# Spline weights from four terms an element; the down weights formed in the feed-forward stage; softmax reciprocals behind the next unit's minima

## The chip, the cores and the metric

One core of a Trainium2 chip runs the whole kernel in one launch. The metric is the device time of an execution in microseconds; a profile is one execution recorded by the hardware profiler. Everything is float32.

## The reference

For four sequences of 512 tokens with 512 features, a layer norm gives `xn`. Two branches read it and both are added to `x`: causal attention with 16 heads of 32 features and a linear position bias (ALiBi), and a gated feed-forward block whose three weights are not stored but interpolated.

```
xn = (x - mean) / sqrt(var + eps)
q, k, v = xn @ W + b                       # 16 heads of 32
p   = softmax(q k^T / sqrt(32) + slope_h * distance, causal)
att = (p v) @ Wo + bo
gate_w, up_w, down_w = catmull_rom(control points)   # 2048x512, 2048x512, 512x2048
ffn = (silu(xn @ gate_w^T) * (xn @ up_w^T)) @ down_w^T
out = x + att + ffn
```

Every spline sample is a sum of four neighbouring control points, each times a cubic of the position. A control point spans about 129 samples, so long runs of a weight row are one cubic. The kernel uses this: it multiplies small factored weights (called `wT` for gate and up, and `dR` and `dM` inside `dRM` for down) with reduced features, which it lays out in DRAM as `table` and loads as `feat`.

## The kernel before, in words

The program is written out as a straight line; each engine carries out its own instructions strictly in the written order (`in_order` ties them so). DMAs are issued by SP (SyncE) and, for the `table` rows, by POOL; an issue that has to wait for an engine or for an earlier transfer holds up all that stands behind it on that queue.

**Attention stage (0 to 388 us).** The work is a list `units` of 64: sequence b, head group hg of four heads, query block i of 128. In iteration n, `scores(units[n])` has PE form four score tiles (L865) in the four PSUM banks of pool `ps_s`, and DVE add the distances and take the row minimum of each (L878, tile `low`); the blocks i = 0 and i = 1 of a group share one set of banks, so their scores are made together. ACT takes the exponentials and their sums (L894). In iteration n+1, `normalize` has DVE form the reciprocals of the four sums (L907, tile `inv`) and POOL multiply the tile by them (L909). In iteration n+2, `swap` transposes part of the tile on DVE (L937) and SP moves it (L945, `move`). In iteration n+3, `turn` transposes the rest on PE (L922), ACT copies it out (L923), and after the group's last block `values` multiplies with v (L966). The banks of `ps_s` come free with DVE's minima, so PE's next scores wait for these. Between them stand the lists `items` (projections L798 and L837, output projections L482, layouts) and `small` (layer norm statistics).

Ahead of `scores(n)` stands `normalize(n-1)`: DVE's reciprocals, which need the sums of ACT, come before the minima of unit n.

**The weights.** `row_weight_steps` forms `wT` in this stage on DVE, as eight terms (`NCG`) for gate and for up: a table `coef` times the control points, a product (L646) and a sum (L649) of 1024 elements a partition each. The points come by four broadcast DMAs a term. `down_steps` forms `dR` and `dM` after that, from five and four terms (L690, L693), with three loads in flight in the space of `feat[0]`. The helper `some_weights` hands out these steps by a budget of microseconds an iteration, half ahead of `items` and half behind; the last step runs at 286 us.

**Feed-forward stage (from 388 us).** The strings in `plans` give the order by hand, one string a sequence. In the first, `G q` and `U q` are the gate and up products of a quarter q on PE (L1135, into the four banks of `ps_g`), `V q` is an up product into the four banks of `ps_o`, `P r` an output projection of the last sequence (L482, one bank of `ps_o`; DVE adds bias and residual, L489, and SP stores it, L492). G is followed by ACT (L1150). U and V are followed by four DVE products a quarter (L1157, tile `inner`), four POOL copies (L1158, tile `made`), and then on SP two exchange DMAs (L1162) and a few small ones (L1167). `F q` loads a quarter of the next `feat` (L549), `X` lets POOL issue rows. In the second string `m0:8` are the first moment products of sequence 0 on PE (L1182); they go into the `ps_o` banks, which V3's four DVE products leave. `down_values` (L1236) is the first to need `dR`.

Of the kernel before, what the change touches and what calls it, by code (L numbers as in the profile page):

```python
# [18 lines left out]
P = 128  # L19
# [29 lines left out]
NCV = 5  # L49
NX = 9 + 4  # L50

COPIES = (1, 1, 4, 1)
NW, NW4 = 11, 4
NST = NW4 + 1

DOWN_STEPS = [("v", lo, hi, c) for lo, hi in ((0, 5), (5, 9)) for c in range(NCV)]
DOWN_STEPS += [("m", 0, NB, c) for c in range(4)]

# [276 lines left out]

def own_points(parts, points):


    values = parts[:, :, :, :9].transpose(0, 4, 3, 1, 2)
    values = values.reshape(P, 9, 2, P // 2, NCD)  # L340
    moments = parts[:, :, :, 9:].transpose(3, 4, 0, 1, 2)
    moments = moments.reshape(P, NB, 2, P // 2, NCD)
    strip = np.broadcast_to(points[:, None, None], (NB, Q32, 9, P, NCD)).reshape(values.shape)
    group = np.broadcast_to(points[None], (P, NB, P, NCD)).reshape(moments.shape)
    own = {}
    for kind, a, number, n in (("v", values, strip, NCV), ("m", moments, group, 4)):
        hit = (a != 0.0).any(axis=3)
        first = np.where(hit.any(axis=3), hit.argmax(axis=3), 0)
        first = np.minimum(first, NCD - n)[:, :, :, None, None] + np.arange(n)
        first = np.broadcast_to(first, (*a.shape[:4], n))  # L350
        few = np.take_along_axis(a, first, axis=4)
        assert np.count_nonzero(few) == np.count_nonzero(a)
        shape = (*a.shape[:2], P, n)
        own[kind] = few.reshape(shape), np.take_along_axis(number, first, axis=4).reshape(shape)
    steps = [[a[:, lo:hi, :, c].reshape(-1) for a in own[k]] for k, lo, hi, c in DOWN_STEPS]
    return *(np.concatenate(a) for a in zip(*steps)),
# [20 lines left out]
_coef = _coef.reshape(NB, NB, P, NCG, 2, Q32).transpose(3, 1, 5, 0, 4, 2)  # L377
COEF = single(_coef.reshape(NCG, P, NB, 2, P))
# [20 lines left out]
def block_kernel(  # L399
# [152 lines left out]
    with ExitStack() as att:  # L552
# [63 lines left out]
        def row_weight_steps(first_down):  # L616
            size = NB * 2 * P
            shaped = lambda a: a.rearrange("p (q x n) -> p q x n", q=NB, x=2)
            spare = [
                feat[0].rearrange("p c h s -> p (c h s)")[:, k * size : (k + 1) * size]  # L620
                for k in range(4)
            ]
            temps = [wd[:, :size], wd[:, size : 2 * size]]
            tabs, points = {}, {}

            def load(c):
                def go():
                    tabs[c], points[c] = (shaped(a) for a in spare[c % 2 * 2 :][:2])
                    nc.sync.dma_start(out=tabs[c], in_=coef[c])
                    for k in range(NB):  # L630
                        strip = slice(k * Q32, (k + 1) * Q32)
                        nc.sync.dma_start(
                            out=spare[c % 2 * 2 + 1][strip],
                            in_=rowpts[c, k].partition_broadcast(Q32),
                        )

                return go

            def term(c, w):
                to = wT[:, :, 2 * w : 2 * w + 2, :]  # L640
                tmp = shaped(temps[w]) if c else to

                def times():
                    own = points[c].rearrange("p (w q) x n -> p w (q x) n", w=2)[:, w]
                    own = own.unsqueeze(2).to_broadcast([P, NB, 2, P])
                    nc.vector.tensor_tensor(tmp, tabs[c], own, ALU.mult)  # L646

                def plus():
                    nc.vector.tensor_tensor(to, to, tmp, ALU.add)  # L649

                return [times, plus] if c else [times]

            steps = [(0.0, load(0)), (0.0, load(1))]
            for c in range(NCG):
                for w in range(2):
                    steps += [(1.2, half) for half in term(c, w)]
                if c + 2 < NCG:
                    steps.append((0.0, load(c + 2)))
                elif c + 2 == NCG:
                    steps += first_down  # L660
            return steps


        def down_steps():
            size = 5 * P
            spare = feat[0].rearrange("p c h s -> p (c h s)")
            given, at = [], 0
            for _, lo, hi, _ in DOWN_STEPS:
                given.append((at, (hi - lo) * P))
                at += P * (hi - lo) * P  # L670

            def load(n):
                def go():
                    at, width = given[n]
                    for k, source in enumerate((downtab, downpts)):
                        to = spare[:, (n % 3 * 2 + k) * size :][:, :width]
                        part = source[at : at + P * width].rearrange("(p x) -> p x", p=P)
                        nc.sync.dma_start(out=to, in_=part)

                return go  # L680

            def term(n):
                kind, lo, hi, c = DOWN_STEPS[n]
                width = given[n][1]
                to = (dR if kind == "v" else dM)[:, lo:hi].rearrange("p a n -> p (a n)")
                tmp = wd[:, n % 2 * size :][:, :width] if c else to
                tab, own = (spare[:, (n % 3 * 2 + k) * size :][:, :width] for k in range(2))

                def times():
                    nc.vector.tensor_tensor(tmp, tab, own, ALU.mult)  # L690

                def plus():
                    nc.vector.tensor_tensor(to, to, tmp, ALU.add)  # L693

                return [times, plus] if c else [times]

            steps = [(0.0, load(n)) for n in range(3)] + [(2.4, lambda: None)]
            for n in range(len(DOWN_STEPS)):
                steps += [(0.9, half) for half in term(n)]
                if n + 3 < len(DOWN_STEPS):  # L700
                    steps.append((0.0, load(n + 3)))
            return steps


# [331 lines left out]
        first_down, *rest = down_steps()  # L1036
        weights = deque(row_weight_steps([first_down]) + rest)
# [27 lines left out]
        for _ in range(2):  # L1065
            weights.popleft()[1]()

        def some_weights(us):
            while weights and us > 0.0:
                cost, step = weights.popleft()  # L1070
                step()
                us -= cost

        for n in range(len(units) + LAG):
            u = units[n] if n < len(units) else None
            old = units[n - LAG] if n >= LAG else None
            if 0 <= n - 1 < len(units):
                normalize(units[n - 1])
            if u:
                scores(u)  # L1080
# [23 lines left out]
            for step in items[n]:  # L1104
                step()
            for step in small[n]:
                step()
# [255 lines left out]
```

## Time and profile before

| | |
|---|---|
| median of 3 runs | 544.58 us (543.7 to 544.58) |
| the profiled execution | 543.63 us, of which 541.4 us are the span from first to last instruction |
| mean granted TensorE clock | 0.993 |
| busy: PE, DVE, ACT, POOL | 530.3, 352.8, 296.0, 243.8 us |
| attention stage, feed-forward stage | 0 to 388 us, 388 to 541 us |
| terms for gate and up (L646, L649) | 30 DVE instructions, 37.5 us, at 44 to 185 us |
| terms for down (L690, L693) | 25 DVE instructions, 19.1 us, at 186 to 287 us |
| loads of the down tables (`feat<-in_downtab`, `feat<-in_downpts`) | 28, of 256 or 320 KB |
| reciprocals (L907) | 64, 10.9 us, and 29.1 us of idle DVE before them until ACT's sums |

A "busy" PE is not PE at its peak: matmuls are pipelined and their ends are modelled, and a matmul that waits for a bank can lie inside a busy stretch. Idle time of another engine costs only where PE then waits for it. In a timeline, instructions of one kind in a row are merged (x4), and the bracket tells how long the engine sat idle before and what ended that.

### The profile page before, as it was taken

Reading aid. Unit: us, or ns where it says so; the run is one execution under the profiler, and the core shown is the slowest. Engines: PE = TensorE matmul, PEld = TensorE weight load, DVE = VectorE, ACT = ScalarE, POOL = GpSimd, SP = SyncE. Lnnn points to the kernel's source line nnn. Section 1 sums busy time; section 2 is a strip of 40 time slices with the busy share of each in tenths; the row PEclk is TensorE's granted clock in tenths of the full one; section 3 lists DMA queues with packets and bytes.
Section 4 is the critical chain, followed back from the end, with each engine's and each line's share of the span. In section 5 each row is a group of like instructions: output and inputs, shape, how many; then the busy total and the mean of one; then the engine's idle time right before and its main releaser. Section 6 shows DMA issues by size and latency. Waiting matters only on the chain.

```text
span 541.4 us, 12182 instructions
## 1 busy us (share of the span) xinstructions
PE 530.3 (98%) x4268; PEld 268.0 (50%) x4268; DVE 352.8 (65%) x990; ACT 296.0 (55%) x798; POOL 243.8 (45%) x436
## 2 busy tenths in 40 slices
PE   7999999999999999999999999989999999999997
PEld 6645545444445544444554454545334555747552
DVE  6169978888677877667676456563135584865836
ACT  2466875665466665646757588883313433624222
POOL 3045635574266565446656567671017232332310
PEclk9999999999999999999999999979999999999999
DMA  8933487575545785745743325464656565665344
GB/s 317 321 122 70 114 213 215 160 194 155 161 144 147 243 276 166 214 142 146 215 123 89 92 67 148 137 188 118 174 165 197 184 221 197 199 203 181 119 164 166
DMA packets 63805, 92.98 MB, mean 172 GB/s; under 512 B 10528, under 2 KB 35104, under 8 KB 63232
## 3 DMA queue, kind: packets, MB, share of 16 engines
q1 hardware_dynamic: 59136, 83.79, 51.5%
q0 software_dynamic: 4608, 8.40, 5.3%
q8 instruction: 34, 0.56, 0.4%
q14 instruction: 27, 0.22, 0.1%
HBM read 50.74 MB, written 23.68 MB: 137 GB/s over the span
## 4 chain that ended last, share of the span: by engine, by line
PE 84%; DVE 5%; DMA 5%; ACT 3%; SPq 2%; issue 1%; DVEq 0%; ACTq 0%
PE mm L798 17%; PE g L1135 9%; PE mm L837 9%; PE s L865 7%; PE mm L922 7%; PE mm L482 6%; PE o L1236 6%; PE c L966 5%; PE o L1182 4%; PE o L1253 3%; PE o L482 3%; ACT p L894 2%; DVE p L878 2%; PE s L482 2%; PE mm L510 2%; PE o L1135 2%
## 5 line engine op out<-in xcount | busy, mean ns | idle before, releaser
L909 POOL TENSOR_SCALAR p<-p,inv 128x128 f32<-128x128 f32 (+3 forms) x256 | 147.5, 589 | 172.1 <-DVE inv L907 122.1
L894 ACT ACTIVATE p<-p,low 128x128 f32<-128x128 f32 (+3 forms) x256 | 141.3, 555 | 48.9 <-DVE low L878 48.3
L878 DVE CUSTOM_DVE_ANT_0 p<-s,dist 128x128 f32<-128x128 f32 (+3 forms) x256 | 108.8, 481 | 21.8 <-PE s L865 21.5
L1158 POOL COPY made<-inner 128x512 f32<-128x512 f32 x64 | 38.9, 637 | 104.2 <-DVE inner L1157 81.5
L923 ACT COPY pT<-mm 128x512 f32<-128x512 f32 x96 | 54.8, 577 | 40.3 <-PE mm L922 40.0
L1135 PE MATMUL g<-feat,wT 32*64 32x512 f32 x864 | 65.3, 592 | 0.0
L1150 ACT ACTIVATE act<-g 128x512 f32<-128x512 f32 x64 | 33.0, 602 | 57.0 <-PE g L1135 56.7
L865 PE MATMUL s<-kT,qT 32*128 32x512 f32 (+3 forms) x512 | 57.4, 479 | 2.2 <-DVE low L878 2.0
L798 PE MATMUL mm<-xnT,wk 128*128 128x512 f32 (+1 forms) x136 | 59.3, 579 | 0.2 <-ACT xnT L783 0.2
L837 PE MATMUL mm<-wv,xnT 128*128 128x512 f32 x128 | 58.1, 596 | 1.1 <-ACT xnT L783 1.1
L798 PE MATMUL mm<-xnT,wq 128*128 128x512 f32 (+1 forms) x136 | 57.8, 567 | 0.0
L922 PE MATMUL mm<-ident,p 128*128 128x128 f32 x384 | 56.5, 283 | 0.4 <-ACT pT L923 0.3
L922 PEld LDWEIGHTS mm<-ident,p 128*128 128x128 f32 x384 | 42.5, 142 | 25.6 <-issue 17.1
L894 ACT ACTIVATION_READ_ACCUMULATOR p<-p,low 128x1 f32 x256 | 48.8, 191 | 0.0
L937 DVE STREAM_TRANSPOSE blocks<-p 128x512 f32<-128x512 f32 x64 | 43.4, 696 | 0.0
L1157 DVE TENSOR_TENSOR inner<-g,act 128x512 f32<-128x512 f32 x44 | 27.3, 683 | 21.7 <-PE g L1135 10.7
L1135 PEld LDWEIGHTS g<-feat,wT 32*64 32x64 f32 x864 | 30.6, 131 | 21.3 <-issue 10.6
L865 PEld LDWEIGHTS s<-kT,qT 32*128 32x128 f32 x512 | 24.5, 186 | 32.8 <-issue 16.2
L798 PEld LDWEIGHTS mm<-xnT,wk 128*128 128x128 f32 x136 | 24.5, 189 | 25.1 <-issue 21.5
L546 POOL DMA_DIRECT2D table<-samples x64 | 36.9, 583 | 0.0
L1236 PE MATMUL o<-inner,dRM 32*64 32x512 f32 x512 | 36.6, 588 | 0.0
L798 PEld LDWEIGHTS mm<-xnT,wq 128*128 128x128 f32 x136 | 24.7, 190 | 22.4 <-issue 21.7
(105 smaller groups left out, 656.3 us busy)
## 6 DMA issues: line engine op xcount, KB each, us to landing
moved<-blocks SPq DMA_DIRECT2D x128, 64.0 KB, 2.1
moved<-blocks SPq DMA_DIRECT2D x64, 128.0 KB, 3.0
feat<-table SPq DMA_DIRECT2D x16, 512.0 KB, 4.3
inner<-made SPq DMA_DIRECT2D x32, 256.0 KB, 3.5
table<-samples POOLq DMA_DIRECT2D x64, 88.0 KB, 3.0
xp<-in_xp_dram SPq DMA_DIRECT2D x16, 256.0 KB, 5.1
feat<-in_coef_dram SPq DMA_DIRECT2D x8, 512.0 KB, 8.8
feat<-in_rowpts_dram SPq DMA_DIRECT2D x32, 128.0 KB, 5.1
```

Of the source, the lines that this page charges most:

```text
L482: nc.tensor.matmul(ps, lhsT=wsb["o"][:, c, r * P : (r + 1) * P], rhs=ctxT[b][:, c, :], start=(c == 0), stop=(c == NB - 1),)
L798: nc.tensor.matmul(ps[0][:, tokens], lhsT=wsb[name][:, c, hg * P : (hg + 1) * P], rhs=xnT[b][:, c, tokens], start=(c == 0), stop=(c == NB ...
L837: nc.tensor.matmul(ps[0], lhsT=xnT[b][:, c, t * P : (t + 1) * P], rhs=wsb["v"][:, c, :], start=(c == 0), stop=(c == NB - 1),)
L865: nc.tensor.matmul(banks[b, hg][j][:, at : at + (k + 1) * P], lhsT=qk[b, hg, "q"][rows, k * P : (k + 1) * P], rhs=qk[b, hg, "k"][rows, : ( ...
L878: nc.vector.tensor_tensor_reduce(out=p[:, j, :nk], in0=ps[j], in1=dists[i % 2][:, S - nk :], scale=-SLOPES[hg * NG + j], scalar=BIG, op0=A ...
L894: nc.scalar.activation(p[:, j, :nk], p[:, j, :nk], AF.Exp, bias=low[:, j : j + 1], scale=-1.0, accum_out=total[:, j : j + 1],)
L909: nc.gpsimd.tensor_scalar(p[:, j, :nk], p[:, j, :nk], inv[:, j : j + 1], 1.0, ALU.mult, ALU.mult)
L922: nc.tensor.transpose(ps[:, j, :], p[:, j, c * P : (c + 1) * P], ident)
L923: nc.scalar.copy(pT[b, hg, c][:, :, (i - c) * P : (i - c + 1) * P], ps)
L937: nc.vector.transpose(own[:, :, k].rearrange("p r j k -> p j r k"), soft[u][0][:, :, c * P : (c + 1) * P].rearrange("p j (r k) -> p j r k" ...
L1135: nc.tensor.matmul(ps[k][cols, :], lhsT=wT[rows, q, 2 * w + part, cols], rhs=feat[b][rows, q, part, :], start=(part == 0), stop=(part == 1),)
L1236: nc.tensor.matmul(sums[b][r][cols, :], lhsT=dR[rows, a, cols], rhs=o[rows, :], start=(a == 0), stop=False,)
```

## The change

1. All weights come from four terms an element (`TAPS`): a new function `own_taps` picks on the host, for each element, the four control points that it has. Gate and up need 8 products and 6 sums on DVE (30 instructions before), with 16 loads of 512 KB (8 of 512 KB and 32 of 128 KB before). Two are loaded ahead; the load for term n+2 is issued at the end of the iteration that holds product n.
2. The steps are handed out by a credit in instructions, not in microseconds, and stand behind `swap` and `move` and ahead of `items`. `move` stands ahead of `items` as well.
3. The down terms leave the attention stage. A generator `down_terms` forms them in 12 products and 9 sums (14 and 11 before) during the first feed-forward string, where the new step `D k` takes k of them. Two terms are loaded ahead, into the `res` and `xp` tiles; the load for term n+2 follows product n.
4. `scores(n)` comes ahead of `normalize(n-1)`, so that DVE's minima of unit n stand ahead of the reciprocals of unit n-1.

```
+def own_taps(a, numbers):
+    first = np.minimum((a != 0.0).argmax(axis=-1), a.shape[-1] - TAPS)
+    own = first[..., None] + np.arange(TAPS)
+    few = np.take_along_axis(a, own, axis=-1)
+    return few, np.take_along_axis(np.broadcast_to(numbers, a.shape), own, axis=-1)
...
+            steps = []
+            for n, (c, w) in enumerate(terms):
                 to = wT[:, :, 2 * w : 2 * w + 2, :]
...
+                tmp = shaped(wd[:, w * size : (w + 1) * size]) if c else to
+                tab, own = (shaped(a) for a in place(n % 2))
+                steps.append(lambda a=(tmp, tab, own): nc.vector.tensor_tensor(*a, ALU.mult))
+                if n + 2 < len(terms):
+                    loads[len(steps)] = load(n + 2)
+                if c:
+                    steps.append(lambda a=(to, to, tmp): nc.vector.tensor_tensor(*a, ALU.add))
...
         for n in range(len(units) + LAG):
...
+            if u:
+                scores(u)
             if 0 <= n - 1 < len(units):
                 normalize(units[n - 1])
-            if u:
-                scores(u)
...
-            budget = 0.0 if n < NB else (1.2, 1.2, 0.6, 1.2)[n % NB] - 0.6 * len(small[n])
-            some_weights(0.5 * budget)
-            for step in items[n]:
-                step()
-            for step in small[n]:
+            move()
+            credit = min(credit + TERMS[n % NB] - 0.25 * len(small[n]), 1.0) if n >= NB else 0.0
+            late = []
+            while done < len(row_terms) and credit > 0.0:
+                row_terms[done]()
+                done += 1
+                credit -= 1.0
+                if done in loads:
+                    late.append(loads[done])
+            for step in (*items[n], *small[n], *late):
                 step()
-            some_weights(0.5 * budget)
-            move()
...
+    def down_terms():
...
+        load(0)
+        load(1)
+        for n, (kind, lo, hi, c) in enumerate(DOWN_STEPS):
+            to = (dR if kind == "v" else dM)[:, lo:hi].rearrange("p a n -> p (a n)")
+            tmp = part(n, 2) if c else to
+            yield
+            nc.vector.tensor_tensor(tmp, part(n, 0), part(n, 1), ALU.mult)
+            if n + 2 < len(DOWN_STEPS):
+                load(n + 2)
+            if c:
+                yield
+                nc.vector.tensor_tensor(to, to, tmp, ALU.add)
...
     last = [proj(B - 1, r, ps_o, "o") for r in range(NB)]
     for load, _ in last[:3]:
         load()
+    terms = down_terms()
+    next(terms)
...
-        "G0 P0 U0 F0 P1 G1 P2 U1 F1 X4 P3 G2 V2 F2 X4 G3 V3 F3",
+        "G0 P0 D2 U0 D1 F0 P1 D2 G1 D1 P2 D2 U1 D1 F1 X4 P3 D2 G2 D2 V2 D1 F2 X4 D2 G3 D2 V3 D3 F3",
```

## The prediction

> **What bounds the kernel now.** I read the page's busy times first, then the stretches of 10 us (columns: width, then busy time and instructions of PE, PEld, DVE, ACT and POOL, the granted TensorE clock, DMA share, GB/s), then the timelines of PE, DVE and SP at the two places where the change acts.
>
> ```profile
> PE 530.3 (98%) x4268; PEld 268.0 (50%) x4268; DVE 352.8 (65%) x990; ACT 296.0 (55%) x798; POOL 243.8 (45%) x436
> ```
> ```profile
> 340.00:350.00 10.00, 10.00 (x70) 4.69 (x68) 4.74 (x19) 7.64 (x24) 6.55 (x14) 1.00 0.58 167
> 350.00:360.00 10.00, 7.62 (x48) 5.06 (x47) 7.51 (x34) 8.73 (x29) 7.91 (x17) 0.84 0.46 116
> 360.00:370.00 10.00, 10.00 (x58) 4.65 (x58) 4.24 (x13) 5.94 (x17) 3.79 (x7) 0.82 0.60 184
> 390.00:400.00 10.00, 10.00 (x72) 3.76 (x79) 3.89 (x6) 2.01 (x4) 2.33 (x4) 1.00 0.59 188
> ```
>
> PE bounds nearly everywhere. It idles 11.1 us in all, 2.4 of them at 350 to 360 us, in the last head group, where no projection is left to cover the softmax. There the granted clock drops too. The timelines of DVE and PE there:
>
> ```profile
> 352.47 0.18 DVE L907 RECIPROCAL inv<-sum 128x4 f32<-128x4 f32 x1 [1.18 <-ACT p L894]
> 354.98 0.18 DVE L907 RECIPROCAL inv<-sum 128x4 f32<-128x4 f32 x1 [0.88 <-ACT p L894]
> ```
> ```profile
> 355.58 2.57 PE L865 MATMUL s<-kT,qT 32*128 32x384 f32 x8 [1.96 <-DVE low L878]
> ```
>
> DVE sits idle before each reciprocal until ACT's sums come, the minima stand behind it, and PE's scores wait for the minima. The first feed-forward string, on DVE and PE, and then on SP:
>
> ```profile
> 394.76 0.75 DVE L489 SCALAR_TENSOR_TENSOR xt<-o,bcol,xt 128x512 f32<-128x512 f32 x1 [6.37 <-DMA xt<-in_xT_dram]
> 395.42 2.48 DVE L1157 TENSOR_TENSOR inner<-g,act 128x512 f32<-128x512 f32 x4
> ...
> 406.45 2.48 DVE L1157 TENSOR_TENSOR inner<-g,act 128x512 f32<-128x512 f32 x4 [1.19 <-PE g L1135]
> ...
> 413.70 2.48 DVE L1157 TENSOR_TENSOR inner<-o,act 128x512 f32<-128x512 f32 x4 [2.91 <-PE o L1135]
> 417.47 2.48 DVE L1157 TENSOR_TENSOR inner<-o,act 128x512 f32<-128x512 f32 x4 [1.28 <-PE o L1135]
> ```
> ```profile
> 418.88 0.61 PE L1182 MATMUL o<-inner,basist 32*64 32x512 f32 x4
> ```
> ```profile
> 389.54 1.88 SPq L477 DMA_DIRECT2D xt<-in_xT_dram  x3
> ...
> 398.61 1.41 SPq L1162 DMA_DIRECT2D inner<-made  x2
> 400.07 2.75 SPq L1167 DMA_DIRECT2D lone<-made  x4
> 403.13 0.34 SPq L549 DMA_DIRECT2D feat<-table  x1
> ...
> 411.15 2.03 SPq L1167 DMA_DIRECT2D lone<-made  x3
> ...
> 419.69 0.58 SPq L549 DMA_DIRECT2D feat<-table  x1
> ```
>
> The four DVE lines of L1157 are the products after U0, U1, V2 and V3. PE takes the next banks only when they are done: G1 after U0, G2 after U1, V3 after V2, and the moments of L1182 after V3. After each come POOL's copies and then six, five or four DMA issues on SP. The last view is the DMA issues (KB each, median us from issue to landing):
>
> ```profile
> feat<-in_downtab_dram SPq DMA_DIRECT2D x9, 256.0 KB, 3.3
> feat<-in_downpts_dram SPq DMA_DIRECT2D x9, 256.0 KB, 3.6
> ```
>
> **Attention stage.** Gate and up lose 16 DVE instructions of 1.2 to 1.3 us, 20 us; the down terms take another 19 us away. DVE is 65% busy and mostly not what PE waits for, so this buys only the short PE stalls of 110 to 240 us: the stretches show 1.7 us of idle PE there, one piece of it a `moved` transfer issued behind a down load. I count 1.5. SP has 28 down loads fewer here, and `move` goes ahead of transfers that nobody waits for soon. Weight terms ahead of `items` cost nothing while DVE has slack (as at 390 us); without it, 1.2 us for each of 14.
>
> The reciprocals: in the last group the minima of unit 60 could start at 351.3, when the transpose ahead of them ends, not at 352.57; those of unit 61 follow at about 353.3 instead of 355.09, so the 1.96 us wait goes. What is late next is the transpose of unit 59, which needs POOL's pass; that starts after ACT's last exponential (352.44) as before and ends at 355.5. Then 1.3 us of transposes, the minima of unit 62 at 357.0 instead of 358.30, unit 63's scores done at 359.8 instead of 362.4 and, after the 3.5 us of output projection, the value products at 363.3 instead of 366.56: 3.2 us. One group earlier a reciprocal holds the minima until 348.17, and PE 0.8 us. So 4.0 us here, 5.5 in all. Against it, POOL's pass starts later by the minima. In the group at 319 us, by the same rows, it would end at 324.9 instead of 322.05, and its first reader started at 325.13: covered, by 0.3 us. Where that fails, the transposes wait and the gain is gone; I bound the stage by -9 and +2.
>
> **Feed-forward stage.** The down terms cost 12 products and 9 sums: by shape 4 x 0.83 + 8 x 0.67 + 3 x 0.91 + 6 x 0.74 = 15.8 us of DVE. DVE idles 18.7 us between 388 and 418 (the sum of the brackets), so the work alone fits. The loads do not. The program's order on SP puts load 4 behind the issues after U0, load 7 behind those after U1, and load 10 behind those after V2, while on DVE products 4, 7 and 10 stand ahead of the L1157 products of U1, V2 and V3. Each is thus a loop: products, POOL copies, exchange issues, load, landing, term, next products. On the clock of the run before:
>
> Start: loads 0 and 1, 1.28 MB, are issued at 391.5 to 393.3 behind three `xt`, of which the first ends DVE's wait at 394.6. At the 300 GB/s of 392 to 394 us they land four microseconds after the last `xt`, at 399.3. Product 1 (0.8) stands ahead of U0's products: 400.1 instead of 395.4, +4.7. Bounds: landing 3.3 after issue gives +1.7; one more microsecond +5.9.
>
> U0 to U1: 395.42 to 403.94 from the products to the end of the store behind F0, then two issues of 0.45, landing 4.1 after the second starts (rows 3.3 to 4.9; F0's 512 KB lie ahead), product 0.67: 13.8 us. Before, 11.0: +2.8 (1.9 to 3.6).
>
> U1 to V2: 406.45 to 413.2 (end of the `lone` issues), then load and product as above, with nothing large ahead and so 3.9: 11.75. Before 7.25: +4.5 (3.9 to 5.6).
>
> V2 to V3: 413.70 to 420.27 (end of F2), the load behind 512 KB of `feat`, 4.4 (up to 5.6), product: 12.1. Before 3.8: +8.3 (7.2 to 9.5).
>
> PE can start the moments when V3's first product has left its bank, 0.7 us before 418.88 in this run: 20.3 - 0.7 = +19.6 (14.0 to 23.9). Nothing behind it gives this back, as PE is full from there to the end. SP's waits for products hold up nothing more: the exchanges behind them wait for later DVE work anyway.
>
> The clock: after a PE idle of 1.96 us the stretches show 0.84 and 0.82, which is 3.4 us of PE lost. PE will now idle some 5 us ahead of V3 and 7 ahead of the moments, and what follows these is PE's own work; I count 2.4 (0 to 3.4). Slow clock at the shorter waits is hidden behind the next load.
>
> *The skill beside the rows.* The Trainium skill (TensorE: Matmul & The Clock Gate, Part 1) gives half clock only after an idle window of about 3.4 us; the row shows it after 1.96 with gaps around it, and by either the two long waits here fall under it, so the sum is 560 by both. The skill's fit for a transfer (DMA: Bandwidth & Descriptors, Anatomy of one DMA; stated for POOL's path) is 2.0 us plus bytes over 436 GB/s, 2.6 us for 256 KB where the rows have 3.3 and 3.6; by it each loop is 1 to 1.5 us shorter and the sum about 556 us.
>
> **Sum.** 543.63 (this execution; its span is 541.4, the median of the runs 544.58) - 5.5 + 19.6 + 2.4 = 560.1; I say 560.
>
> **Rivals.**
> *The loads land in time (faster).* Then only the order of DVE's work costs: 3.5 us of terms ahead of V3's products, where DVE idled 1.28 and PE had 0.7 to spare, +1.5. 543.6 - 5.5 + 1.5 = 539.6. It decides if load 4 lands before PE's P2 ends (404.5) and load 10 before 416. For it speak the 18.7 us of idle DVE and the DMA share of 0.59; against it, SP cannot issue load 4 before 403.9. Chance 0.06.
> *Everything late (slower still).* With the upper landing times, the whole loss of clock and attention gaining nothing: 543.6 + 23.9 + 3.4 + 0 = 571. For it: a transfer of 256 KB at 413 us sits in a DMA share of 0.86. Chance 0.14.
> *The normal case at the lower ends*, landing 3.3 everywhere, no clock lost, attention -9: 548.6. It lies in the forecast's 0.79.
> *Same.* The losses would have to equal the gains, 5 to 6 us, under the lower bound of the loops: 0.01.
>
> **How the numbers follow.** A difference under about 0.2% (1.1 us) cannot be told from none. Slower holds 0.79 + 0.14 = 0.93, same 0.01, faster 0.06. The range 550 to 569 leaves out the faster rival, the last microsecond at the low end and the top of the late case, some 0.18.
>
> **What would show it.** In the changed kernel's profile: DVE's L1157 products (its L1097) with idle up to 10 us ahead of the terms, ended by DMA `res<-in_downtab` or `in_downpts`; distances between the four groups near 14, 12 and 12 us; PE idle ahead of V3 and of the first moments and a clock under 1.00 behind; the value products of the last group 3 us sooner after the one before; no reciprocal with DVE idle and minima behind it. I am wrong if the terms' loads end no DVE wait, or if the L1157 groups keep their old distances.

## The result and the profile after

The changed kernel takes 568.88 us (median of 4 runs, 568.18 to 569.35), the kernel before 544.41 us beside it (4 runs, 543.7 to 544.58): 4.5% slower, ratio 1.0451 with an interval of 1.0433 to 1.0469. The profiled execution took 568.18 us with a span of 566.0 us. The forecast was 560 us in a range of 550 to 569: the median lies 0.1 us under its top.

The page's busy times and its row of the granted clock:

```profile
PE 543.4 (96%) x4268; PEld 280.0 (49%) x4268; DVE 337.7 (60%) x970; ACT 295.3 (52%) x798; POOL 242.3 (43%) x436
PEclk9999999999999999999999999699798799999999
```

DVE has 15 us less to do and the kernel is 24.6 us longer: DVE's work was not what the time hung on. The timeline of DVE in the first feed-forward string (L1229 are the down products, L1097 the four products after U0, U1, V2 and V3):

```profile
397.66 0.82 DVE L1229 TENSOR_TENSOR dRM<-res 128x640 f32<-128x640 f32 x1 [3.11 <-DMA res<-in_downpts_dram]
...
400.06 2.48 DVE L1097 TENSOR_TENSOR inner<-g,act 128x512 f32<-128x512 f32 x4
...
415.07 2.48 DVE L1097 TENSOR_TENSOR inner<-g,act 128x512 f32<-128x512 f32 x4
...
426.19 0.69 DVE L1229 TENSOR_TENSOR xp<-xp 128x512 f32<-128x512 f32 x1 [5.10 <-DMA xp<-in_downpts_dram]
426.80 2.48 DVE L1097 TENSOR_TENSOR inner<-o,act 128x512 f32<-128x512 f32 x4
...
440.38 0.69 DVE L1229 TENSOR_TENSOR res<-res 128x512 f32<-128x512 f32 x1 [5.99 <-DMA res<-in_downpts_dram]
440.99 2.47 DVE L1097 TENSOR_TENSOR inner<-o,act 128x512 f32<-128x512 f32 x4
```

The groups stand 15.0, 11.7 and 14.2 us apart where they stood 11.0, 7.25 and 3.8. The last two are each ended by a load, as the brackets say. The issues on SP behind U0, U1 and V2 (L1221 are the loads of the down terms; load 4 goes to `res`, load 7 to `xp`, load 10 to `res`):

```profile
408.25 0.33 SPq L551 DMA_DIRECT2D feat<-table  x1
...
409.58 0.47 SPq L1221 DMA_DIRECT2D res<-in_downpts_dram  x1
...
422.83 0.52 SPq L1221 DMA_DIRECT2D xp<-in_downpts_dram  x1
...
433.61 0.58 SPq L551 DMA_DIRECT2D feat<-table  x1
...
434.80 0.43 SPq L1221 DMA_DIRECT2D res<-in_downpts_dram  x1
```

PE's view of the same (G0, then G1, V3 and the first moments):

```profile
387.26 1.97 PE L1075 MATMUL g<-feat,wT 32*64 32x512 f32 x32
...
400.80 5.47 PE L1075 MATMUL g<-feat,wT 32*64 32x512 f32 x32 [2.40 <-DVE inner L1097]
406.20 6.64 PE L484 MATMUL o<-wd,wo 128*128 128x512 f32 x8
...
427.54 4.62 PE L1075 MATMUL o<-feat,wT 32*64 32x512 f32 x30 [3.21 <-DVE inner L1097]
441.73 1.12 PE L1122 MATMUL o<-inner,basist 32*64 32x512 f32 x2 [7.13 <-DVE inner L1097]
```

The projection P2, in the line behind G1, took 6.64 us, at half clock; P3, at 414.67 us and full clock, took 3.70. G0 in the kernel before:

```profile
387.81 1.97 PE L1135 MATMUL g<-feat,wT 32*64 32x512 f32 x32
```

The bookkeeping of the two spans, in three pieces: the attention stage ends (first G product) at 387.26 instead of 387.81, -0.55; from there to the moments it is 54.47 instead of 31.07, +23.40; behind them 124.27 instead of 122.52, +1.75. Together +24.6.

### The profile page after: what moved, and what is told of

It reads as the page before. It is cut to its first block, busy times and chain, and to the rows that moved or that the text cites. A ratio compares the mean times of both kernels' runs of the same rounds, so it can differ in the third digit from the quotient of the medians.

```text
span 566.0 us, 12139 instructions
## 1 busy us (share of the span) xinstructions
PE 543.4 (96%) x4268; PEld 280.0 (49%) x4268; DVE 337.7 (60%) x970; ACT 295.3 (52%) x798; POOL 242.3 (43%) x436
## 4 chain that ended last, share of the span: by engine, by line
PE 85%; DMA 5%; DVE 4%; POOL 2%; SPq 2%; issue 1%; ACT 0%; DVEq 0%; POOLq 0%
PE mm L742 19%; PE mm L781 10%; PE s L809 8%; PE g L1075 8%; PE mm L866 8%; PE o L1176 5%; PE mm L484 5%; PE c L910 5%; PE o L1122 4%; DMA xp<-in_downpts_dram 3%; PE o L1193 3%; PE mm L512 2%; PE s L484 2%; PE o L484 2%; POOL p L853 1%; PE g L1122 1%
## 5 line engine op out<-in xcount | busy, mean ns | idle before, releaser
L853 POOL TENSOR_SCALAR p<-p,inv 128x128 f32<-128x128 f32 (+3 forms) x256 | 144.5, 577 | 174.8 <-DVE inv L851 145.6
L822 DVE CUSTOM_DVE_ANT_0 p<-s,dist 128x128 f32<-128x128 f32 (+3 forms) x256 | 109.5, 483 | 62.3 <-PE s L809 62.2
L1098 POOL COPY made<-inner 128x512 f32<-128x512 f32 x64 | 40.7, 661 | 127.3 <-DVE inner L1097 102.5
L1075 PE MATMUL g<-feat,wT 32*64 32x512 f32 x864 | 71.0, 611 | 2.4 <-DVE inner L1097 2.4
L1075 PEld LDWEIGHTS g<-feat,wT 32*64 32x64 f32 x864 | 35.6, 136 | 24.0 <-issue 9.6
L1097 DVE TENSOR_TENSOR inner<-g,act 128x512 f32<-128x512 f32 x44 | 27.3, 682 | 19.5 <-PE g L1075 15.4
L1176 PE MATMUL o<-inner,dRM 32*64 32x512 f32 x512 | 38.2, 588 | 0.0
L1122 PE MATMUL o<-inner,basist 32*64 32x512 f32 x384 | 29.7, 631 | 7.1 <-DVE inner L1097 7.1
```

What stands on the lines that cost most here:

```text
L822: nc.vector.tensor_tensor_reduce(out=p[:, j, :nk], in0=ps[j], in1=dists[i % 2][:, S - nk :], scale=-SLOPES[hg * NG + j], scalar=BIG, op0=A ...
L853: nc.gpsimd.tensor_scalar(p[:, j, :nk], p[:, j, :nk], inv[:, j : j + 1], 1.0, ALU.mult, ALU.mult)
L1075: nc.tensor.matmul(ps[k][cols, :], lhsT=wT[rows, q, 2 * w + part, cols], rhs=feat[b][rows, q, part, :], start=(part == 0), stop=(part == 1),)
L1122: nc.tensor.matmul(own[b][r][half * ND : (half + 1) * ND, :], lhsT=basist[rows, g + half, :], rhs=inner[b, g + half][rows, :], start=(g == 0),
L1176: nc.tensor.matmul(sums[b][r][cols, :], lhsT=dR[rows, a, cols], rhs=o[rows, :], start=(a == 0), stop=False,)
```

## Experiments

Ratios are against the kernel before, run again beside the experiments: its medians are 546.42 us beside experiments 1 to 3, 543.98 beside 4 to 7, 544.46 beside 9 and the first kernel of 8, and 544.83 beside the second of 8. A "slow stretch" is one in which the profile shows TensorE at half clock; experiment 5 is about these.

**1. The down terms alone.** Which part of the change makes the loss? The kernel before with part 3 only: eight-term rows and the old order of the reciprocals stay.

```
-        first_down, *rest = down_steps()
-        weights = deque(row_weight_steps([first_down]) + rest)
+        weights = deque(row_weight_steps())
...
+    terms = down_terms()          # as in the change, with its first string
+    next(terms)
```

> The kernel before with the down terms alone moved to the first feed-forward string as in the change; eight terms for gate and up, old order of the reciprocals. Theory (the move of the down terms is the whole loss): 567 to 571 us. Rival (the three parts interact, the attention parts lose too): 560 to 565 us.

Measured 569.8 us, ratio 1.0419 (1.0357 to 1.0480). Moving the down terms alone loses as much as the whole change (1.0451). Its groups stand 15.9, 11.9 and 14.1 us apart, as in the changed kernel.

**2. The changed kernel without most of the down loads.** Ten of the twelve pairs of loads are left out, so that the terms use old data and the output differs; all DVE work stays.

```
-            if n + 2 < len(DOWN_STEPS):
-                load(n + 2)
```

> The changed kernel with ten of the twelve pairs of down loads left out (the terms are formed from what lies in the tiles, in the same places and as many); what is left is the wait for loads 0 and 1 and the order of DVE's work. Theory (loads issued on SP behind the exchange come late): V2's products follow U1's after 7 to 8.5 us, V3's follow V2's after 4 to 6.5; 552 to 557 us. Rival (the 15.8 us of DVE terms ahead of the products are the cause): 565 us or more, distances as in the changed kernel.

Measured 553.06 us, ratio 1.0111 (1.0060 to 1.0162): 15.8 us less than the changed kernel: most of the loss comes from the loads. In its profile the distances are 14.8, 7.2 and 6.0 us. Two stay short, as expected. U0 to U1 stays long although no load is waited for; there DVE waits for PE, and PE has a slow stretch: its L484 took 6.58 us. So two causes lie side by side at this place, and taking one away shows the other; experiment 5 takes away the other one.

**3. The reciprocals alone, and all but the reciprocals.** The edit of the first, on the kernel before; the second undoes the same lines in the changed kernel.

```
+            if u:
+                scores(u)
             if 0 <= n - 1 < len(units):
                 normalize(units[n - 1])
-            if u:
-                scores(u)
```

> The kernel before with scores(n) ahead of normalize(n-1) and nothing else. Theory (the order saves DVE's wait, but the last head group then gets its time eaten by a slow clock, as in the changed kernel, where it kept 0.6 of 2.6 us): 542 to 544.5 us. Rival (the prediction's hand schedule holds once the other parts are away: 4 us in the last group): 540.5 us. Rival (POOL's later pass makes the transposes wait): above 545 us. In the trace: the 1.96 us of PE ahead of the scores at 355 us gone in all three but the last.

> The changed kernel with normalize(n-1) ahead of scores(n) again. If the new order of the reciprocals is worth something in the attention stage: 569 to 571.5 us, the first feed-forward string unchanged. If it costs: 566 us or less. If the loss is all in the first feed-forward string, its distances between the four groups of products (15.0, 11.7 and 14.2 us) stay within half a microsecond either way.

On the kernel before, this alone gives 542.95 us, ratio 0.9942 (0.9908 to 0.9975): inside the theory's range, and the best of all kernels here. The gain may be smaller than 0.6%, as the kernel before scattered beside it (542.33 to 549.89 us) and had medians of 544.0 to 544.8 at the other times. The changed kernel with the old order has 568.25 us, ratio 1.0387 (1.0328 to 1.0445), with groups 15.8, 12.2 and 14.3 us apart; next to the changed kernel's own 1.0451 (1.0433 to 1.0469) at another time, the reordering gained nothing there. The traces say why. With all but the reciprocals, the minima of the unit at 344 us come 2.71 us earlier than before; with the reciprocals too, 0.62. (On the kernel before, the new order alone brings them 0.69 us earlier.) Of the 2.1 us, 1.1 are lost between 214 and 242 us and most of the rest at 331. Around 228 us a row product on DVE ran beside POOL's pass and took 3.69 us (1.2 to 1.6 elsewhere). That is not the whole cause: in experiments 6 and 7, whose attention code is the same, the product takes 1.2 us there and the same 1.1 us are lost, with a PE wait of 0.7 us for ACT's copy of the transposed tile; why is open. From the timelines at 331 us, first of the changed kernel, then of the one with the old order, which stood 1.4 us ahead by then:

```profile
320.77 3.65 POOL L853 TENSOR_SCALAR p<-p,inv 128x512 f32<-128x512 f32 x4 [1.68 <-DVE inv L851]
321.11 1.42 DVE L644 TENSOR_TENSOR wT<-wT,wd 128x1024 f32<-128x1024 f32 x1
324.45 1.30 DVE L881 STREAM_TRANSPOSE blocks<-p 128x512 f32<-128x512 f32 x2 [0.46 <-POOL p L853]
330.93 0.85 PE L910 MATMUL c<-moved,v 128*32 128x384 f32 x8 [1.11 <-DMA moved<-blocks]
```
```profile
322.42 1.30 DVE L881 STREAM_TRANSPOSE blocks<-p 128x512 f32<-128x512 f32 x2
328.60 0.85 PE L910 MATMUL c<-moved,v 128*32 128x384 f32 x8 [0.21 <-issue]
```

The reciprocal stands behind the minima and POOL's pass behind the reciprocal. There the pass now lies beside a row sum on DVE (L644): one of its four instructions takes 1.64 us where the others take 0.68, and the pass 3.65. DVE's stream transpose waits for POOL, the `moved` transfer leaves later, and the value products wait for it: 2.33 us apart now. With the reciprocals alone, on the kernel before, whose last weight step runs at 286 us, the same pass takes 2.69 us. The transposes start at 324.45 us there too, after a wait of 0.86, but that is earlier than the 325.13 of the kernel before. From the timelines of these two, first the kernel before:

```profile
319.35 2.70 POOL L909 TENSOR_SCALAR p<-p,inv 128x512 f32<-128x512 f32 x4 [1.57 <-DVE inv L907]
325.13 1.30 DVE L937 STREAM_TRANSPOSE blocks<-p 128x512 f32<-128x512 f32 x2
```
```profile
321.72 2.69 POOL L909 TENSOR_SCALAR p<-p,inv 128x512 f32<-128x512 f32 x4 [2.48 <-DVE inv L907]
324.45 1.30 DVE L937 STREAM_TRANSPOSE blocks<-p 128x512 f32<-128x512 f32 x2 [0.86 <-POOL p L909]
```

**4. The reciprocals behind the minima in the last head group only.**

```
-            if u:
+            if u and n >= len(units) - NB:
                 scores(u)
             if 0 <= n - 1 < len(units):
                 normalize(units[n - 1])
+            if u and n < len(units) - NB:
+                scores(u)
```

> The changed kernel with the reciprocals behind the next minima in the last head group alone (the last four units). Theory (in the groups before, the later reciprocal delays POOL's pass, the stream transposes and the moved transfer, which cost 1.4 to 2.1 us): scores of the last group but one unit start near 350.7 us, 2.3 earlier than with the reorder everywhere, and the stage ends 1.5 to 2.3 us earlier as long as the clock does the same; 566 to 567 us. Rival (the reorder costs nothing in the earlier groups): 568 us, and the minima of unit 60 begin no earlier than 350.0.

Measured 566.39 us, ratio 1.0405 (1.0367 to 1.0442). The theory holds for the stage: it ends at 382.50 us, 4.8 earlier than in the changed kernel. 1.6 us of these are there when the last group begins; the other 3.2 are the last group's, which has no slow stretch here (16.4 us from one group's value products to the next, 19.6 in the changed kernel). Of the 4.8 us, 2.9 reach the end, as the string behind stands at its loads: 7.4 us of PE idle ahead of the moments and 15.1, 11.9 and 15.2 us between the groups.

**5. The clock.** I cut the profiles into stretches as long as the shortest complete slow one, 3.413 us. In each of the 14 profiles all slow stretches begin on one fixed grid of this step, which lies elsewhere in each, and those that the execution's end does not cut are 1 to 4 steps long. Here the grid falls as follows at the end of the attention stage (columns: width, busy time and instructions of PE, PEld, DVE, ACT and POOL, granted clock, DMA share, GB/s); the first fence is the changed kernel, the second the one with the reciprocals alone:

```profile
350.71:354.12 3.41, 2.67 (x16) 1.76 (x15) 2.76 (x17) 3.41 (x15) 3.37 (x7) 1.00 0.40 104
354.12:357.54 3.42, 3.42 (x15) 2.01 (x12) 2.32 (x7) 2.91 (x11) 3.37 (x8) 0.50 0.40 95
357.54:360.95 3.41, 3.41 (x10) 1.91 (x10) 2.31 (x10) 3.23 (x10) 2.46 (x6) 0.50 0.75 190
360.95:364.37 3.42, 3.42 (x5) 1.35 (x5) 1.28 (x5) 1.67 (x6) 2.63 (x6) 0.50 0.82 282
```
```profile
350.04:353.45 3.41, 2.67 (x19) 1.78 (x16) 2.61 (x15) 3.41 (x14) 3.37 (x7) 1.00 0.52 138
353.45:356.86 3.41, 2.48 (x16) 1.56 (x14) 2.29 (x10) 3.19 (x11) 3.37 (x8) 1.00 0.47 93
```

Both kernels run the same work here at the same times to 0.1 us, with the same 2.67 us of busy PE. Only the grid lies 0.67 us apart, and one is slow for three stretches and the other for none. What tells them apart, as far as I can count it, is PE's work in a stretch, each matmul counted at its spacing at full clock (128x512: eight per 3.44 us; a tile of fewer rows and columns by its share of the array): 37% of the stretch in the first, 43% in the second. Over all 14 profiles, the 63 stretches that a slow one follows hold 0 to 38%, the 2150 that none follows 36% and more: the two overlap a little, as the ends of matmuls are modelled. At half clock a stretch can hold about half of that work at most, so a wait inside a slow one easily brings another.

The test: matmuls that nobody reads, where PE would idle.

```
+            for j in range(3 if b == B - 1 and hg == NHG - 1 else 0):
+                nc.tensor.matmul(ps[:, j, :], lhsT=ident, rhs=ident, start=True, stop=True)
             for j in range(NG):                      # transposes of turn()
...
-        "G0 P0 D2 U0 D1 F0 P1 D2 G1 ... G3 D2 V3 D3 F3",
-        "G0 m0:8 ...
+        "G0 P0 D2 U0 D1 F0 P1 o4 D2 G1 ... G3 g5 D2 V3 D3 F3",   # 4 and 5 matmuls of 128x512
+        "G0 g12 m0:8 ...                                         # 12 of them
```

> The changed kernel with matmuls whose result nobody reads, where PE would idle: three of 128x128 ahead of each group of transposes of the last head group, four of 128x512 ahead of G1, five ahead of V3, twelve ahead of the first moments. Theory (a stretch of 3.413 us with PE's work under about 0.38 of a full stretch is followed by one at half clock): no stretch at 0.5 remains or only one; P2 takes 3.7 us and not 6.6, so that U0 to U1 is 13.8 us, set by load 4, and not 15.0; the last group saves some 2 to 3 us and the moments 1.7. In all 3 to 6 us off 568.3: 562 to 565 us. Rival (the clock follows something other than PE's work, or the added work costs what it saves): 568 us or more, with stretches at 0.5 in the same places.

One slow stretch is left, mean clock 0.996 (0.973 without), and P2 takes 3.70 us: the clock follows PE's work. The time does not follow: 570.2 us, ratio 1.0485 (1.0450 to 1.0521), as in the rival's second half, where the added work costs what it saves. The fill in the transposes behind the out-projections met no idle PE and cost 4 us: from the value products of the last group to G0 it is 25.3 us instead of 21.2. And U0 to U1 stayed at 15.1 us, now ended by load 4:

```profile
415.20 0.69 DVE L1231 TENSOR_TENSOR dRM<-res 128x512 f32<-128x512 f32 x1 [4.63 <-DMA res<-in_downpts_dram]
```

I had expected 13.8 there, as the prediction had. In the changed kernel load 4 landed at 414.37 and its product began at 414.46: load and half clock ended together.

**6. The loads on ACT's queue.**

```
-                nc.sync.dma_start(out=part(n, k), in_=given)
+                nc.scalar.dma_start(out=part(n, k), in_=given)
```

> The changed kernel with the down loads issued on ACT's queue, so that none stands behind the exchange issues of SP. Theory (the order on SP delays the loads): load 7 can be issued when its slot is freed, at about 418.3 us and not at 422.26, and lands 3.5 us later, V2's products at 422.5 instead of 426.80; load 10 at about 426 instead of 434.29, V3's products at 430.5 to 432 instead of 440.99. U1's products stay at 415, as PE's P2 ends last there. In all 9 to 10 us off 568.3: 558 us. Rival (the landing time in a busy DMA sets the distances, wherever the loads are issued): distances U1 to V2 and V2 to V3 stay at 11 us or more, 566 us or more.

Measured 559.19 us, ratio 1.0295 (1.0228 to 1.0361). The total is near the expected 558, its parts are not: U0 to U1 fell to 10.6 us, which I had not expected, and the next two stayed at 12.1 and 11.5, as the rival said. V2's products waited for load 7, and load 7 for the slot that load 5 fills; load 5 was issued at 407.18, 3.4 us earlier than in the changed kernel, but landed 7.3 us after that and not 5.1, in a DMA share of 1.04 (410 to 415 us). So the order on SP makes one part of the loss, and transfers that share DMA the other. The Trainium skill (DMA: Bandwidth & Descriptors, Issuing engines are not separate DMA queues) says that all issuing engines' transfers run on the same 16 DMA engines and that a second queue saves only issue time; the two distances that stayed agree with it. From G0 to the moments it is 46.4 us all the same, where the changed kernel has 54.5: these 8 us are what the waits ahead of the loads on SP had cost, with the half clock behind them. ACT's own work pays for it: the silu of G3 stands behind load issues, and PE waits 4.17 us for it.

**7. Five slots.** Five terms in flight in tiles that stand idle here, and the terms behind the products of U0 and U1.

```
-            return spare[n % 2][:, k * size :][:, : (hi - lo) * P]
+            return spare[n % 5][:, k * size :][:, : (hi - lo) * P]
...
-        load(0)
-        load(1)
+        for n in range(5):
+            load(n)
...
-            if n + 2 < len(DOWN_STEPS):
-                load(n + 2)
+            if n + 5 < len(DOWN_STEPS):
+                load(n + 5)
...
+        "G0 P0 U0 F0 P1 D5 G1 P2 D1 U1 F1 X4 P3 D4 G2 V2 D1 F2 X4 G3 V3 D6 F3",
+        "G0 m0:8 U0 D4 L F0 ...
```

> The changed kernel with five load slots instead of two (three tiles more that stand idle in this string), five terms loaded ahead, and the terms placed behind the products of U0 and U1 in DVE's order. Theory (each late product waits for one load that could not be issued earlier): no product group waits for a load; the distances of the four groups go back to about 11, 7.3 and 4 to 5 us, and the time to 543 to 546 us. Rival (15.8 us of terms on DVE, or 7.5 MB of loads in DMA, do not fit in this string however they are placed): 552 us or more.

Measured 555.3 us, ratio 1.0212 (1.0176 to 1.0247): in the rival's range, if for another reason. Start and U0 to U1 are back (7.6 and 11.1 us), U1 to V2 is 12.9:

```profile
417.90 0.69 DVE L1231 TENSOR_TENSOR res<-res 128x512 f32<-128x512 f32 x1 [5.87 <-DMA res<-in_downpts_dram]
```

Its load follows a product that ended at 400.4; SP issued it at 410.83, behind the exchange of U0, F0 and a store. Seven issues in a row, from 393.43 to 398.47 us, began 0.02 to 0.07 us after the landing of the transfer eight issues before on that queue. The trace names eight completion counters that the transfers use in rotation: with five pairs of loads, SP stood waiting for a free counter. So the store of P0 went out at 398.47 us (394.58 in the changed kernel) and landed at 404.51; the next load into its tile waited for that, and the exchange stood behind it.

**8. Five slots and ACT's queue, in two placements.** First all loads on ACT; then the first five on SP, the rest on ACT behind the silu of G1, G2 and G3, with the reciprocals as in experiment 4.

```
-        "G0 P0 U0 F0 P1 D5 G1 P2 D1 U1 F1 X4 P3 D4 G2 V2 D1 F2 X4 G3 V3 D6 F3",
+        "G0 P0 U0 F0 P1 G1 D5 P2 D1 U1 F1 X4 P3 G2 D4 V2 D1 F2 X4 G3 V3 D6 F3",   # first
+        "G0 P0 U0 F0 P1 G1 D5 P2 D1 U1 F1 X4 P3 G2 D4 V2 F2 X4 G3 D1 V3 D6 F3",   # second
...
+                nc.scalar.dma_start(out=part(n, k), in_=given)                     # first
...
+            queue = nc.sync if n < 5 else nc.scalar                                # second
```

> The kernel with five load slots, its loads issued on ACT's queue behind the silu of G1 and of G2. In the one before it, product 5 waited 5.87 us for a load that its slot allowed at 400.4 and SP issued at 410.83. Theory (what is left of the loss is the order on SP): that load is issued near 403.5 and lands by 410, U1 to V2 goes back to 7.3 to 8.5 us, and the time to 546 to 549 us. Rival (6.8 MB in 35 us beside the other transfers fill DMA, whatever the queue): U1 to V2 or V2 to V3 stays 4 us too long, 552 us or more.

> Five load slots; the first five loads on SP, the later seven on ACT's queue behind the silu of G1, G2 and G3, so that no silu stands behind a load that waits; reciprocals behind the next minima in the last head group alone. Theory (the loss of the change is made by loads that are issued late, on whichever queue, and the attention stage gains where the later reciprocal delays no transfer): feed-forward starts 4 to 5 us earlier than in the kernel before, the four product groups stand 11, 7.3 and 4 to 5 us apart, and the time is 539 to 542 us, under both kernels. Rival (6.8 MB of loads beside the other transfers do not fit whatever the queue): one of the distances stays 4 us too long, 545 us or more.

The first has 563.02 us, ratio 1.0344 (1.0322 to 1.0367). U1 to V2 is 7.25 us, as the theory wanted. But the third load on ACT was issued only at 393.91, 0.02 us after a `feat` transfer of SP's had landed, and the first silu stands behind it and its followers (it starts at 398.24, after 11.14 us): U0's products begin at 402.67, which by the profile a load's landing ended; why they wait for that one is open. V2 to V3 is 8.3 us, 4.5 too long, as the rival said, but by a silu: it stands behind an issue that waited until 431.92 for a `feat` transfer. The second has 552.55 us, ratio 1.0136 (1.0102 to 1.0170). It starts U0's products at 391.24, 4.2 us ahead of the kernel before, keeps U0 to U1 at 11.1 us, and then loses it all in one wait. The waits of ACT, 400 to 420 us (total, times, longest), and its timeline:

```profile
ACT act L1092 <- DMA ctxT<-in_downpts_dram: 18.5, 1, 18.5
```
```profile
407.44 0.39 ACTq L1226 DMA_DIRECT2D ctxT<-in_downtab_dram  x1
414.98 0.33 ACTq L1226 DMA_DIRECT2D ctxT<-in_downpts_dram  x1
```

The issue at 414.98 began 0.02 us after the landing of the `feat` transfer that SP had issued at 406.37 on the same counter: both queues share the counters. Silu, V2's products and PE (8.47 us idle) stood behind it. U1 to V2 is 15.6 us, longer than the rival asked for. Both of my cases failed in part: what is left is neither the order on SP nor the DMA rate alone, but a counter that the loads wait for, and an engine's own work that waits behind them.

**9. The down terms back in attention, with four terms.** Part 3 of the change undone; first with the old order of the reciprocals, then with that of experiment 4.

```
+        weights = deque()
+        for k, step in enumerate(row_terms, 1):
+            weights.append((1.2, step))
+            if k in loads:
+                weights.append((0.0, loads[k]))
+        weights += down_steps()
```

> The changed kernel with the down terms (four each now) back in the attention stage behind the row terms, with the budget of the kernel before, and the reciprocals where they were: of the change only the shorter sums and the earlier move are left. Theory (the short sums themselves give what the attention stage gained; with the down terms moved alone unit 59 came 0.45 us earlier, with the short row sums too 2.7 us): the minima of unit 59 come 2 to 2.5 us earlier than in the kernel before, the feed-forward stage as before, 541.5 to 542.3 us where the kernel before has 544. Rival (the gain came from taking the down terms out of the stage): 543.5 to 544.5 us.

> The same with the reciprocals behind the next minima in the last head group alone. Theory (there, and only there, the later reciprocal takes a PE wait away and delays nothing): the last scores start 1.5 to 2 us earlier than without, and the half clock behind the 1.96 us wait goes as well: 538 to 540 us. Rival (the gain in the last group is given back by POOL's pass and the value products): 541.5 us or more.

551.89 us (ratio 1.0148, 1.0121 to 1.0174) and 551.11 us (1.0116, 1.0095 to 1.0137): neither theory; of the rivals the first does not hold, and the second (541.5 us or more) by its number alone. The loss of 8 us lies at 70 to 117 us. Waits in the first, 60 to 145 us:

```profile
DVE wd L640 <- DMA feat<-in_rowpts_dram: 5.6, 2, 3.2
DVE dRM L673 <- DMA feat<-in_downpts_dram: 5.1, 1, 5.1
```

A four-term row product needs 1 MB and comes at the old pace, and the first down loads, issued at 109.5 behind `moved` transfers, stand directly ahead of their product; minima and PE (3.60 us idle) wait behind it. It is the mistake of the change in another stage. What four-term rows are worth with the down terms in this stage stays open. With the reciprocals of experiment 4 the last group began 1.3 us later in that profile and its last minima came 2.9 us earlier; but a slow stretch made the output projection behind them 5.40 us long instead of 3.70, and the value products came 0.6 us later. The medians are 0.8 us apart, the other way.

## Why the prediction was right, step by step

*The sign and the main mechanism* held: the terms' loads are late, the products wait for them, PE waits for the products. Experiments 1 and 2 show it.

*Start*: +4.7 predicted, +5.2 from G0 to U0's products. Right.

*U0 to U1*: 13.8 predicted, 15.0 measured. The load's second issue starts 9.5 us after U0's products and not 9.0, and it lands 4.8 us later and not 4.1. "Slow clock at the shorter waits is hidden behind the next load" was right for the time, if barely: P2 ran at half clock, and experiment 5 took that away without shortening the distance.

*U1 to V2*: 11.75 predicted, 11.73 measured, with the issue 0.5 us later and the landing 0.6 us sooner (3.3).

*V2 to V3*: 12.1 predicted, 14.2 measured: the issue is 1.0 us later, and landing takes 5.5 us where I took 4.4, close to my bound of 5.6. The bound was the better estimate: the load stood behind 512 KB of `feat` with DMA at 0.84 to 0.86. Together +23.4 from G0 to the moments, where +19.6 (14.0 to 23.9) was predicted. None of the three loads landed as fast as the 2.6 us that the prediction sets beside its rows.

*The clock*: 2.4 (0 to 3.4) predicted behind the two long waits; +1.75 measured behind the moments, where a slow pair of stretches reaches from 439.45 to 446.28 us.

*Attention* is the term that was mis-sized: -5.5 predicted, -0.55 measured. Its pieces: the short sums and the missing down terms gave -2.7 (1.5 predicted; the down terms alone, experiment 1, -0.45); the reordering cost +2.1 ahead of the last group (-0.8 predicted); in the last group it gave nothing in this execution, 19.56 us from one group's value products to the next instead of 19.48 (-3.2 predicted). The value products, in the kernel before, in the changed kernel and with the reciprocals alone:

```profile
347.08 1.07 PE L966 MATMUL c<-pT,v 128*32 128x512 f32 x8
...
366.56 1.06 PE L966 MATMUL c<-pT,v 128*32 128x512 f32 x8
```
```profile
346.46 1.06 PE L910 MATMUL c<-pT,v 128*32 128x512 f32 x8
...
366.02 1.06 PE L910 MATMUL c<-pT,v 128*32 128x512 f32 x8
```
```profile
346.38 1.06 PE L966 MATMUL c<-pT,v 128*32 128x512 f32 x8
...
363.08 1.06 PE L966 MATMUL c<-pT,v 128*32 128x512 f32 x8
```

Two steps failed. One is "covered, by 0.3 us". The reader was the right one: 325.13 is DVE's stream transpose in the kernel before. But the pass was priced at the 2.7 us that it takes there, where no weight step runs any more at 321 us. The shorter sums of parts 1 and 2 are spread up to 321 us, a row sum now lies beside the pass, and it takes 3.65. On the kernel before, where none does, the reordering alone gave 0.7 ahead of the last group, as predicted. The case I named for a failure ("the gain is gone") is what happened. The other step is the last group: I let the half clock there go together with the 1.96 us wait. That wait went (0.30 us are left of it), and the half clock stayed, as it depends on PE's work in a stretch of the grid and not on one wait. The 16.70 us with the reciprocals alone have no slow stretch; that profile is the fastest of ten runs (540.35 us, median 542.95). At the same number of slow stretches no gain shows: with one, 18.2 us in the old order (the second kernel of experiment 3) and 18.1 to 18.4 in the new (experiment 6, the second kernels of 8 and 9); with two, 18.8 to 19.5 in the old (the kernel before, experiment 1, the first of 9) and 19.5 in the new (experiment 2). No profile has the old order and no slow stretch. Whether the new order makes slow stretches rarer stays open.

The errors add up: 5.0 us less gain and 3.8 more loss, less 0.7 of clock, are the 8.1 us by which this execution (568.18) stands above the 560.1 of the sum. In its pieces the result (+23.4, +1.75, -0.55) is nearer to the rival "everything late" (+23.9, +3.4, 0; 571 us, chance 0.14) than to the forecast (+19.6, +2.4, -5.5). The direction and the mechanism were argued; that the median still lies inside the range, by 0.1 us, is in part luck.

## What to carry to other kernels

Work moved onto an idle engine carries its loads along: ask on which queue they are issued, what stands ahead of them there, and what on the engine stands behind their first use. More slots or another queue help only until the next thing in order, an engine's own work or a completion counter, stands behind a waiting issue. When two parts of a change are priced on the profile of before, ask what each moves beside the other: the later POOL pass was covered there, and no longer once the row sums of the other part ran beside it.

## What the runs showed of the hardware

- The half clock comes in whole stretches of 3.413 us on a fixed grid, after a stretch in which PE's work was under some 37% of a full one (0 to 38%, against 36% and more ahead of a fast one; experiment 5). PE need not stand idle: 2.67 of 3.41 us were busy ahead of the three slow stretches. The Trainium skill (TensorE: Matmul & The Clock Gate, Part 1) gives the free-running window of 3413 ns, which all profiles here confirm, and names an idle window as the trigger, which the runs extend to a window with little work. The same attention code ran in five profiles here (the changed kernel and experiments 2, 6, 7 and the first of 8) with 3, 2, 1, 3 and 0 slow stretches in the last group, and that group took 19.6, 19.5, 18.4, 19.6 and 16.7 us. That is up to 2.9 us between executions of the same attention code, in step with the slow stretches. The ten runs of one program, the reciprocals alone, go from 540.35 us at a mean clock of 1.000 to 545.57 at 0.989.
- Transfers issued by SP and ACT share eight completion counters: an issue waits for the landing of the earlier transfer that used the same one. In the first string of the changed kernel no issue is held by it; in experiments 6 to 8 some are, for up to 7.2 us.
- Where a DVE product or sum of 128x1024 ran beside POOL's pass, one of the two took longer: the product 3.69 us instead of 1.2 (at 228 us in the changed kernel and in experiment 5), or the pass 3.65 to 3.76 instead of 2.69 (there in experiments 2, 6, 7 and the first of 8, and at 321 us in the changed kernel). In the kernel with the old order the pair met at 228 us too, and there the pass took 3.66 us and the product 1.6.
